# Seven block products for eight in the retention projections of a decoder layer

## The chip, the cores and the metric

The kernel runs on one core of one Trainium2 chip. Five engines work side by side, each with its own queue of instructions, taken in order: TensorE (PE, matrix products), VectorE (DVE), ScalarE (ACT), GpSimd (POOL) and SyncE (SP), which here starts all transfers. The metric is the time of one execution on the device, in microseconds (us); lower is better.

## The reference

One decoder layer with norms after the sums, for 8 batches of 100 tokens of width 1024, all in float32: retention with 8 heads, then attention to a context of 722 tokens per batch and the own tokens, then a gated feed-forward layer. The change touches the retention:

```python
q = (hidden_states @ Wq).reshape(B, T, H, DK)      # H = 8, DK = 128
k = (hidden_states @ Wk).reshape(B, T, H, DK)
v = (hidden_states @ Wv).reshape(B, T, H, DV)      # DV = 256
g = (hidden_states @ Wg).reshape(B, T, H, DV)
q = _rope(q)
k = _rope(k)
...
scores = jnp.einsum('bihd,bjhd->bhij', q * scale, k) * D[None]
o = jnp.einsum('bhij,bjhd->bihd', scores, v)
rms = jax.lax.rsqrt(jnp.mean(o * o, axis=-1, keepdims=True) + EPS)
o = o * rms * g_norm_weight
o = o * (g * jax.nn.sigmoid(g))
return o.reshape(B, T, H * DV) @ Wo
```

## The kernel before

The 800 tokens are worked in two halves of 400 (`N`), with features on the 128 partitions and tokens along the free dimension. A weight block of 1024 x 128 lies as eight 128 x 128 tiles side by side (`KT` = 8), and eight matmuls of 400 columns add up in one PSUM accumulator.

Float32 precision is kept by splitting. `split` writes an operand as a rounded part and a rest: a cast on ScalarE (line 69), then a subtraction on VectorE (line 70). `mm3` (lines 88 to 90) forms one product from three matmuls: high x high, high x low, low x high. `load_w` brings 512 KB of a weight block into a raw tile `wst` (3 buffers) and splits it into a tile `w` (4 buffers). `proj` forms one block for one half: 24 matmuls.

The retention stage first loads x, as pairs of k tiles (`xs`), and splits it into four `big` tiles, two for each half of the tokens, one for each half of the 1024 contraction rows. Then it goes over the 8 heads. A head takes six weight blocks: q, k, two of v and two of the gate. Each of the six is multiplied with both halves. q and k pass through `rope` (VectorE, lines 134 to 137, straight from PSUM). v is copied out by ScalarE and turned by four TensorE transposes (`tokens_first`). Scores (line 349), their decay (350), the products with v (356), the squares and their sums follow. Then a block of the context weights `wc[h]` is split and stored to DRAM for a later stage (`wcd`), the gate blocks are formed and passed through Silu, and `inv_root` with a sum over partitions on GpSimd (`all_red`, line 125) scales the result, which is split into `of` and stored to DRAM (`o1d`). The output projection and layer norm (`out_proj`) follow, which reload `o1d` into the `big` tiles. PSUM has three accumulators with tag `a`, four with `s` and one with `v`.

Later come the second attention and the feed-forward stage. The latter already forms its products in sevens (`seven`, by Strassen's sums), which prepares weight quarters by sums (`w_pair`, line 631), copies products out on ScalarE (line 659) and adds them on VectorE (line 663).

The order in which instructions stand on each engine is not that of the source: a scheduler interleaves independent work when the program is built, within what tiles, buffers and dependences allow. Waits between engines go by semaphores that it sets.

Of the kernel before, what the change touches and what calls it, by code (L numbers as in the profile page):

```python
# [8 lines left out]
F32 = mybir.dt.float32  # L9
# [19 lines left out]
T6 = T - R6            # first token that sees keys of chunk 6  # L29
N6 = 4 * R6            # scores of chunk 6, of the tokens that see its keys  # L30
NH1 = 8                # heads of the first attention
NKV = 4                # kv heads of the second
NHID = 32              # blocks of the hidden width
UNITS = NHID // 2      # pairs of hidden blocks
LAST = 3               # pairs of the last down projection
CUT = 5 * T            # tokens in the first of the two parts that are normed last
# [5 lines left out]
def decoder_layer(ctx, tc, xT, cT, w1, wo1, w2, wo2, wc, w3, wd, gw, qw, kw, trig, dec, mask, out):  # L42
# [21 lines left out]
    def split(dst, src):  # L64
        """dst[:, 0] + dst[:, 1] == src, each with the 12 significant bits that one pass takes."""
        split2(dst[:, 0], dst[:, 1], src)
# [20 lines left out]
    def mm3(acc, lh, ll, rh, rl, start, stop):  # L87
        nc.tensor.matmul(acc, lh, rh, start=start, stop=False)  # L88
        nc.tensor.matmul(acc, lh, rl, start=False, stop=False)  # L89
        nc.tensor.matmul(acc, ll, rh, start=False, stop=stop)  # L90
# [20 lines left out]

    def inv_root(pool, ss, eps, n=N):
        """-2 (ss + eps)^-1/2: by exp(-ln/2), then a Newton step."""
        r = pool.tile([P, n], F32, tag="r0", name="r0")
        nc.scalar.activation(r, ss, AF.Ln, bias=eps)  # L115
        nc.scalar.activation(r, r, AF.Exp, scale=-0.5)  # L116
        q = pool.tile([P, n], F32, tag="r1", name="r1")
        nc.scalar.activation(q, r, AF.Square)
        nc.vector.scalar_tensor_tensor(q, ss, eps, q, ALU.add, ALU.mult)  # L119
        nc.vector.scalar_tensor_tensor(q, q, 3.0, r, ALU.subtract, ALU.mult)  # L120
        return q
# [6 lines left out]
    def rope(pool, acc, cosw, sinw, tag="t1"):  # L128
        """acc * cos + (acc with its halves swapped) * sin."""
# [10 lines left out]
    def tokens_first(pool, acc):  # L140
        """[128, 4 x 100] -> PSUM [100, 4 x 128]: the transposes of the four batches."""
        vt = pool.tile([P, N], F32, tag="vt", name="vt", bufs=1)
        nc.scalar.copy(vt, acc)
        tr = bank("s")
        for b in range(NB):
            nc.tensor.transpose(tr[0:T, b * P:(b + 1) * P], vt[:, b * T:(b + 1) * T], ident)
        return tr[0:T]

# [1 line left out]
    o1d = dr.tile([NH1, P, 2, 2, 2, N], FR, name="o1d")            # head, p, half, block, hi/lo, token  # L150
# [11 lines left out]
    def big(shape):  # L162
        return bp.tile(shape, FR, tag="big", name="big")

# [28 lines left out]
    def load_constants(p, trg):  # L193
# [6 lines left out]
        # rotary tables with the norm weights of q and k; factors left over from inv_root  # L200
# [7 lines left out]
    def out_proj(half, w, load_o, res, yp, ybufs, p, make_z, dst, after=None):  # L208
        """res + o @ w of one half, then its layer norm: split for the next products, and to dst."""
# [71 lines left out]
    # A norm with little left to do once the last block of rows is there: all blocks are taken relative to the mean  # L281
    # of the others, so that the mean of what they then hold, delta, is that of the last block alone, and the
    # variance is mean(y^2) - delta^2 (delta^2 is at most an eighth of mean(y^2)).
# [24 lines left out]
    with sbuf("l1", 2) as p:  # L308
        x = []
        for half in range(2):  # L310
            z = [big([P, 2, QT, N]) for _ in range(2)]
            if half == 0:
                w0 = load_w(w1[0, 0], parts=4)
            for k in range(0, KT, 2):
                xs = p.tile([P, 2, N], F32, tag="xs", name="xs", bufs=4)
                nc.sync.dma_start(out=xs, in_=xT[half, :, k:k + 2])
                for i in range(2):
                    split(z[k // QT][:, :, k % QT + i], xs[:, i])
            if half == 0:
                wk0 = load_w(w1[0, 1])  # L320
                trg = p.tile([P, 4, T], F32, name="trg", bufs=1)
                nc.sync.dma_start(out=trg, in_=trig)
            x.append(z)
        dcy = load_constants(p, trg)

        for h in range(NH1):
            qk = [[None, None], [None, None]]
            for i in range(2):
                w = (w0, wk0)[i] if h == 0 else load_w(w1[h, i])
                for half in range(2):  # L330
                    t = rope(p, proj(w, x[half]), trg[:, 2 * i], trg[:, 2 * i + 1], f"qk{i}")
                    qk[i][half] = t
            v = [[None, None], [None, None]]
            for blk in range(2):
                w = load_w(w1[h, 2 + blk])
                for half in range(2):
                    tr = tokens_first(p, proj(w, x[half]))
                    vv = p.tile([T, NB * P], F32, tag=f"v{blk}", name="vv")
                    nc.scalar.copy(vv, tr)
                    v[half][blk] = vv  # L340
            # scores with their decay, and o^T
            oo, sq = [[None, None], [None, None]], [[None, None], [None, None]]
            for half in range(2):
# [7 lines left out]
                for blk in range(2):  # L351
# [6 lines left out]
                    s_ = p.tile([P, N], F32, tag=f"sq{blk}", name="sq")  # L358
# [4 lines left out]
            # a block of the context weights, split once for all batches  # L363
            w = load_w(wc[h])
            nc.sync.dma_start(out=f32(wcd[h]), in_=f32(w))
            wg = [load_w(w1[h, 4 + blk]) for blk in range(2)]
            g = [[None, None], [None, None]]
            for half in range(2):
                for blk in range(2):
                    gs = p.tile([P, N], F32, tag=f"g{blk}", name="gs")  # L370
                    nc.scalar.activation(gs, proj(wg[blk], x[half]), AF.Silu)
                    g[half][blk] = gs
            ln_exp()
            for half in range(2):
                r = inv_root(p, all_red(p, sq[half][0], "ss"), eps_o)
                for blk in range(2):
# [3 lines left out]
                    of = p.tile([P, 2, N], FR, tag="of", name="of")  # L380
# [46 lines left out]
    y2pool = sbuf("y2", 1)  # L427
    y2p = y2pool.__enter__()
    with sbuf("cx", 2) as p, sbuf("c1", 1) as p1:
        for b in range(B):  # L430
# [10 lines left out]
            for kv in range(NKV):  # L441
                # K^T of the context, to be scaled by its norms when the scores leave PSUM, and V
# [29 lines left out]
                # -2 / norm of the context keys, keys on partitions  # L472
# [14 lines left out]
                # scores, keys on partitions, and their maximum  # L487
# [23 lines left out]
                # exponentials, split, and their sum  # L511
# [27 lines left out]
                # 1 / sum: exp(-ln), then a Newton step (the sum is 1 or more)  # L539
# [22 lines left out]
    # [C11 C12; C21 C22] = [A11 A12; A21 A22] [B11 B12; B21 B22] by Strassen's seven products; the rows of A  # L562
    # are two blocks of one weight, the columns of B the two halves of the tokens
# [53 lines left out]
    H = QT * P  # L617

    def load_raw(src):
        st = wp.tile([P, KT * P], F32, tag="wst", name="wst", bufs=3)  # L620
        nc.sync.dma_start(out=st, in_=src)
        return st

    def w_pair(*ops):
        """Two of the sums of quarters of a weight, split; a sum goes to the first quarter's place unless that is kept."""
# [15 lines left out]
    def seven(i, part, t0=None):  # L641
        """Two blocks of the gate (part 0) or of the other factor (part 1): C11, C12, C21, C22."""
# [24 lines left out]
        add(s2, s2, s4)                                     # C21  # L667
# [6 lines left out]
        add(s4, s4, prod(t2, 1, "b11+b12"))                 # C22  # L674
        m5 = prod(t3, 0, "b22")
        add(s1, s1, m5, ALU.subtract)                       # C11
        add(s3, s3, m5)                                     # C12
        return s1, s3, s2, s4

    # the first two blocks by all eight products: half of them need the first half of the tokens alone  # L680
# [13 lines left out]
    with sbuf("ff", 1) as p:  # L694
# [59 lines left out]
        # the last rows are normed in two parts  # L754
# [16 lines left out]
def _chunks(w, n):  # L771
    """[K, M] -> [M / 128, K / (n 128), 128, n 128]: k tiles of 128 x 128 side by side."""
# [66 lines left out]
```

## Time and profile before

| | us |
|---|---|
| median of 3 runs | 2617.55 (2616.77 to 2619.95) |
| span of the profiled execution | 2615.0 |
| TensorE busy in it | 2552.7 (98%) |
| VectorE busy | 1922.2 (74%) |
| ScalarE busy | 1256.3 (48%) |
| GpSimd busy | 466.3 (18%) |
| matmuls | 14438 |

The span reaches from the first to the last instruction of the one execution that was profiled; the page gives no other time for that execution, and the median of the timed runs lies 2.55 us above its span. The retention stage takes about the first 500 us. Group rows read: line, engine, operation, written tile <- read tiles, shapes and count | busy us, mean ns of one | idle time before them and what ended it. Matmuls overlap each other, so the mean of one is longer than the distance between two starts. A row of windows gives the busy us of each engine in a stretch, with the number of instructions, the granted TensorE clock, the busy share of the DMA engines and GB/s.

### The profile page before, as it was taken

The page shows a single profiled execution, that of the slowest core. Times are in us where ns is not written, and L with a number is a line of the kernel's source. Part 1 is how long each engine was busy: PE and PEld are TensorE (multiplying, and loading weights), DVE is VectorE, ACT ScalarE, POOL GpSimd, SP SyncE. Part 2 cuts the span into 40 slices and gives each one's busy share as a digit, 9 for nine tenths or more (in the row PEclk, how much of TensorE's full clock was granted, in tenths as well). Part 3 has the DMA queues.
Part 4 walks back from the last instruction along what each step waited for, and adds up shares of the span by engine and source line. Part 5 has one row for each costly group of instructions (what it writes and reads, how often), then busy time and mean ns, then how long its engine had stood idle before and what let it go on. Part 6 is the DMA issues. An engine that isn't in the chain of part 4 may idle for free.

```text
span 2615.0 us, 37589 instructions
## 1 busy us (share of the span) xinstructions
PE 2552.7 (98%) x14438; PEld 2511.4 (96%) x14438; DVE 1922.2 (74%) x3201; ACT 1256.3 (48%) x2202; POOL 466.3 (18%) x222
## 2 busy tenths in 40 slices
PE   8999999999998899999999999999999999999998
PEld 8999999999998899999999999999999999999996
DVE  4454554456999888888988989866866766866885
ACT  4555544533555455655655566533433433423351
POOL 0010000000544434434333343100000000000000
PEclk9999999999999999999999999999999999999999
DMA  5323333664434644544554553564421211211221
GB/s 173 98 98 119 100 117 122 214 241 154 144 133 138 236 158 137 188 158 146 174 166 139 185 173 113 210 245 143 146 73 65 73 57 65 81 50 64 70 84 51
DMA packets 157233, 346.44 MB, mean 132 GB/s; under 512 B 45018, under 2 KB 95578, under 8 KB 147838
## 3 DMA queue, kind: packets, MB, share of 16 engines
q1 hardware_dynamic: 157054, 344.05, 39.5%
q8 instruction: 113, 1.85, 0.3%
q14 instruction: 66, 0.54, 0.1%
HBM read 279.81 MB, written 64.19 MB: 132 GB/s over the span
## 4 chain that ended last, share of the span: by engine, by line
PE 80%; DVE 10%; ACT 6%; issue 3%; DMA 2%; SPq 0%; DVEq 0%; ACTq 0%
PE a L88 16%; PE a L90 16%; PE a L89 16%; PE s L88 8%; PE s L89 8%; PE s L90 8%; PE v L88 3%; PE v L90 2%; PE v L89 2%; DVE r L119 1%; ACT L116 1%; ACT L115 1%; PE s L469 1%; DVE ot L378 1%; DVE t L136 1%
## 5 line engine op out<-in xcount | busy, mean ns | idle before, releaser
L88 PE MATMUL a<-big,w 128*128 128x400 f32 (+2 forms) x2300 | 778.5, 339 | 17.1 <-ACT big L69 9.5
L89 PE MATMUL a<-big,w 128*128 128x400 f32 (+2 forms) x2300 | 779.7, 339 | 0.0
L90 PE MATMUL a<-big,w 128*128 128x400 f32 (+2 forms) x2300 | 778.3, 339 | 0.0
L88 PEld LDWEIGHTS a<-big,w 128*128 128x128 f32 x2300 | 432.4, 188 | 20.6 <-ACT big L69 9.8
L90 PEld LDWEIGHTS a<-big,w 128*128 128x128 f32 x2300 | 433.9, 189 | 0.6
L89 PEld LDWEIGHTS a<-big,w 128*128 128x128 f32 x2300 | 433.1, 188 | 1.1 <-DVE big L70 0.5
L69 ACT CAST w<-wst 128x1024 fp32r<-128x1024 f32 (+2 forms) x300 | 259.2, 869 | 346.6 <-PE a L90 152.6
L70 DVE TENSOR_TENSOR w<-wst,w 128x1024 fp32r<-128x1024 f32 (+2 forms) x300 | 303.7, 1015 | 164.8 <-ACT w L69 163.2
L125 POOL PARTITION_ALL_REDUCE ss<-sq x56 | 157.3, 2817 | 725.4 <-DVE sq L362 442.3
L459 POOL PARTITION_ALL_REDUCE kss<-ksq x64 | 171.6, 2682 | 141.2 <-ACT ksq L458 140.7
L69 ACT CAST w<-as 128x512 fp32r<-128x512 f32 x90 | 55.9, 621 | 215.3 <-PE a L90 180.9
L88 PE MATMUL s<-big,w 128*128 128x400 f32 x428 | 150.4, 352 | 2.5 <-ACT big L69 2.5
L89 PE MATMUL s<-big,w 128*128 128x400 f32 x428 | 149.4, 349 | 1.6 <-DVE big L70 1.6
L90 PE MATMUL s<-big,w 128*128 128x400 f32 x428 | 148.8, 348 | 0.0
L505 ACT ACTIVATE s<-s,rk 128x400 f32<-128x400 f32 x160 | 88.0, 591 | 97.3 <-DVE sm L527 63.3
L663 DVE TENSOR_TENSOR s<-s 128x400 f32<-128x400 f32 x183 | 102.4, 569 | 25.3 <-ACT s L659 19.5
L125 POOL PARTITION_ALL_REDUCE mb<-sm x32 | 83.3, 2603 | 201.1 <-DVE sm L527 201.1
L524 ACT ACTIVATE s<-s 128x800 f32<-128x800 f32 (+1 forms) x128 | 95.1, 750 | 41.0 <-DVE s L518 38.1
L70 DVE TENSOR_TENSOR pl<-s,ph 128x800 fp32r<-128x800 f32 (+1 forms) x128 | 108.3, 850 | 2.5 <-ACT ph L69 2.0
L506 DVE TENSOR_TENSOR mx<-mx,s 128x400 f32<-128x400 f32 x128 | 80.5, 629 | 26.5 <-ACT s L505 23.3
L88 PE MATMUL a<-z,w 128*128 128x400 f32 x192 | 70.5, 367 | 24.0 <-DVE t L136 22.9
L69 ACT CAST ph<-s 128x800 fp32r<-128x800 f32 (+1 forms) x128 | 92.4, 731 | 0.9
(269 smaller groups left out, 5605.6 us busy)
## 6 DMA issues: line engine op xcount, KB each, us to landing
wst<-in_w SPq DMA_DIRECT2D x137, 512.0 KB
w<-wcd SPq DMA_DIRECT2D x64, 1024.0 KB
wst<-in_wo SPq DMA_DIRECT2D x64, 512.0 KB
wst<-in_wd SPq DMA_DIRECT2D x32, 512.0 KB
o1d<-of SPq DMA_DIRECT2D x32, 400.0 KB
big<-o1d SPq DMA_DIRECT2D x16, 800.0 KB
qd<-d SPq DMA_DIRECT2D x32, 400.0 KB
q<-qd SPq DMA_DIRECT2D x32, 400.0 KB
```

Of the source, the lines that this page charges most:

```text
L69: nc.scalar.copy(hi, src)
L70: nc.vector.tensor_tensor(lo, src, f32(hi), ALU.subtract)
L88: nc.tensor.matmul(acc, lh, rh, start=start, stop=False)
L89: nc.tensor.matmul(acc, lh, rl, start=False, stop=False)
L90: nc.tensor.matmul(acc, ll, rh, start=False, stop=stop)
L115: nc.scalar.activation(r, ss, AF.Ln, bias=eps)
L125: nc.gpsimd.partition_all_reduce(y, x, P, op)
L459: nc.gpsimd.partition_all_reduce(ss[:, at], sq[:, at], P, RED.add)
L505: nc.scalar.activation(sc, sp, AF.Copy, scale=rk[:, c:c + 1])
L506: nc.vector.tensor_tensor(mx, s[:, 1] if j == 2 else mx, sc, ALU.max)
L524: nc.scalar.activation(e, e, AF.Exp)
L663: nc.vector.tensor_tensor(t, x, y, op)
```

## The change

The two weight blocks of a pair (q and k, the two of v, the two of the gate) are taken as two rows of a 2 x 2 block matrix, whose columns are the two halves of the contraction. x is the other 2 x 2 block matrix: rows are the contraction halves, columns the token halves. The four blocks of the product then take seven block products, in the Winograd form of Strassen's method, for eight. For head 0, q and k stay as they were.

Four differences of the quarters of x (`t1` to `t4`) are formed and split once, from a second load of x. `t1`, `t2` and `t3` get tiles of their own; `t4` takes the `big` tile of quarter b12, which the seven products don't read. For each pair, four sums of weight quarters are formed on VectorE, and 3 1/2 tiles of split weights for two. Some products add onto an accumulator that already holds an earlier one, after ScalarE has copied out that earlier one; three sums on VectorE finish the blocks. One of the four blocks of a pair stays in PSUM, so three of the four copies ahead of the transposes go.

Besides, x is loaded in blocks of one k tile into a pool of ten tiles `tp`, which also holds the copied products; the sum over partitions moves ahead of the gate; the squares `sq` and the tile `of` get one buffer for two. Apart from removed comments, the rest is unchanged.

```diff
+    def wino_weights(pool, src0, src1):
+        r0, r1 = load_raw(src0), load_raw(src1)
+        a11, a12, a21, a22 = r0[:, :H], r0[:, H:], r1[:, :H], r1[:, H:]
+        ta = w_split(r0)
+        v = pool.tile([P, 2 * H], F32, tag="ws", name="ws", bufs=1)
+        nc.vector.tensor_tensor(v[:, :H], a21, a22, ALU.add)
+        nc.vector.tensor_tensor(a21, a11, a21, ALU.subtract)
+        tb = w_split(r1)
+        nc.vector.tensor_tensor(a11, v[:, :H], a11, ALU.subtract)
+        td = w_split(a11)
+        nc.vector.tensor_tensor(v[:, H:], a12, a11, ALU.subtract)
+        return dict(A11=(ta, 0), A12=(ta, 1), S3=(tb, 0), A22=(tb, 1), S2=(td, 0)), v
+
+    def wino(pool, src0, src1, zb, temp, tags):
+        w, v = wino_weights(pool, src0, src1)
+        x, y, z = (bank(t)[:, :N] for t in tags)
...
+        prod(x, "A11", "b11")
+        p1 = copied(x)
+        prod(y, "S3", "t3")
+        p7 = copied(y)
+        prod(x, "S2", "t2", start=False)
+        u2 = copied(x)
+        prod(z, "A12", "b21")
+        nc.vector.tensor_tensor(p1, z, p1, ALU.add)
+        tc_ = w_split(v)
+        w["S1"], w["S4"] = (tc_, 0), (tc_, 1)
+        prod(x, "S1", "t1", start=False)
+        nc.vector.tensor_tensor(p7, x, p7, ALU.add)
+        prod(y, "A22", "t4", start=False)
+        nc.vector.tensor_tensor(u2, y, u2, ALU.add)
+        prod(x, "S4", "b22", start=False)
+        return p1, x, u2, p7
...
+        qk0 = [[proj(w, x[half]) for half in range(2)] for w in (w0, wk0)]
+        for name in ("t1", "t2", "t3"):
+            zb[name] = p.tile([P, 2, QT, N], FR, tag="zt", name=name, bufs=3)
+        zb["t4"] = big([P, 2, QT, N])
+        for k in range(QT):
+            r = {}
+            for name, half, kk in (("b11", 0, k), ("b12", 1, k), ("b21", 0, QT + k), ("b22", 1, QT + k)):
+                r[name] = temp()
+                nc.sync.dma_start(out=r[name], in_=xT[half, :, kk])
+            def mixed(name, dst, a, b):
+                nc.vector.tensor_tensor(r[dst], r[a], r[b], ALU.subtract)
+                split(zb[name][:, :, k], r[dst])
...
+            mixed("t3", "t3", "b22", "b12")
+            mixed("t1", "b12", "b12", "b11")
+            mixed("t2", "b22", "b22", "b12")
+            mixed("t4", "b21", "b21", "b22")
...
-            for i in range(2):
-                w = (w0, wk0)[i] if h == 0 else load_w(w1[h, i])
-                for half in range(2):
-                    t = rope(p, proj(w, x[half]), trg[:, 2 * i], trg[:, 2 * i + 1], f"qk{i}")
-                    qk[i][half] = t
+            for half, i in ((0, 0), (1, 1), (0, 1), (1, 0)):
+                qk[i][half] = rope(p, acc[i][half], trg[:, 2 * i], trg[:, 2 * i + 1], f"qk{i}")
+            c11, c12, c21, c22 = wino(p, w1[h, 2], w1[h, 3], zb, temp, "asa")
...
+                ss.append(all_red(p, sq[half][0], "ss"))
...
-            wg = [load_w(w1[h, 4 + blk]) for blk in range(2)]
+            c11, c12, c21, c22 = wino(p, w1[h, 4], w1[h, 5], zb, temp, "asa")
...
-                    of = p.tile([P, 2, N], FR, tag="of", name="of")
+                    of = p.tile([P, 2, N], FR, tag="of", name="of", bufs=1)
```

More of the change, by code (lines that the diff above doesn't have):

```diff
@@ L85, in load_ws, with mm3 @@
         return w
[L87 to L90, printed above, removed]
+    def mm3(acc, lh, ll, rh, rl, start, stop, chain=False):
+        nc.tensor.matmul(acc, lh, rh, start=start, stop=False, skip_group_check=chain)
+        nc.tensor.matmul(acc, lh, rl, start=False, stop=False, skip_group_check=chain)
+        nc.tensor.matmul(acc, ll, rh, start=False, stop=stop, skip_group_check=chain)
     def mmw(acc, w, k, rh, rl, start, stop):
@@ L138, in rope, with tokens_first @@
         return t1
-    def tokens_first(pool, acc):
-        vt = pool.tile([P, N], F32, tag="vt", name="vt", bufs=1)
-        nc.scalar.copy(vt, acc)
+    def tokens_first(pool, acc, copied=True):
+        vt = acc
+        if copied:
+            vt = pool.tile([P, N], F32, tag="vt", name="vt", bufs=1)
+            nc.scalar.copy(vt, acc)
         tr = bank("s")
@@ L305, in norm_late, with load_raw, w_split @@
         scaled(y, r, dst, z)
+    H = QT * P
+    def load_raw(src):
+        st = wp.tile([P, KT * P], F32, tag="wst", name="wst", bufs=3)
+        nc.sync.dma_start(out=st, in_=src)
+        return st
+    def w_split(src):
+        w = wp.tile([P, 2, KT * P], FR, tag="w", name="w", bufs=4)
+        split(w[:, :, :src.shape[1]], src)
+        return w
+    def wino_weights(pool, src0, src1):
[10 more added lines that the diff above has]
+        return dict(A11=(ta, 0), A12=(ta, 1), S3=(tb, 0), A22=(tb, 1), S2=(td, 0)), v
@@ new lines, in wino, with prod, copied @@
+    def wino(pool, src0, src1, zb, temp, tags):
+        w, v = wino_weights(pool, src0, src1)
+        x, y, z = (bank(t)[:, :N] for t in tags)
+        def prod(acc, a, b, start=True, stop=True):
+            t, c = w[a]
+            for k in range(QT):
+                e = slice(c * H + k * P, c * H + (k + 1) * P)
+                mm3(acc, t[:, 0, e], t[:, 1, e], zb[b][:, 0, k], zb[b][:, 1, k],
+                    start and k == 0, stop and k == QT - 1, True)
+        def copied(acc):
+            t = temp()
+            nc.scalar.copy(t, acc)
+            return t
+        prod(x, "A11", "b11")
[14 more added lines that the diff above has]
+        return p1, x, u2, p7
@@ L308, in decoder_layer, with temp @@
     with sbuf("l1", 2) as p:
-        x = []
+        def temp():
+            return p.tile([P, N], F32, tag="tp", name="tp", bufs=10)
+        zb = {}
         for half in range(2):
-            z = [big([P, 2, QT, N]) for _ in range(2)]
+            zb["b1%d" % (half + 1)], zb["b2%d" % (half + 1)] = big([P, 2, QT, N]), big([P, 2, QT, N])
             if half == 0:
                 w0 = load_w(w1[0, 0], parts=4)
-            for k in range(0, KT, 2):
-                xs = p.tile([P, 2, N], F32, tag="xs", name="xs", bufs=4)
-                nc.sync.dma_start(out=xs, in_=xT[half, :, k:k + 2])
-                for i in range(2):
-                    split(z[k // QT][:, :, k % QT + i], xs[:, i])
+            for k in range(KT):
+                xs = temp()
+                nc.sync.dma_start(out=xs, in_=xT[half, :, k])
+                split(zb["b%d%d" % (k // QT + 1, half + 1)][:, :, k % QT], xs)
@@ L322, in decoder_layer @@
                 nc.sync.dma_start(out=trg, in_=trig)
-            x.append(z)
+        x = [[zb["b11"], zb["b21"]], [zb["b12"], zb["b22"]]]
         dcy = load_constants(p, trg)
-        for h in range(NH1):
-            qk = [[None, None], [None, None]]
-            for i in range(2):
-                w = (w0, wk0)[i] if h == 0 else load_w(w1[h, i])
-                for half in range(2):
-                    t = rope(p, proj(w, x[half]), trg[:, 2 * i], trg[:, 2 * i + 1], f"qk{i}")
-                    qk[i][half] = t
-            v = [[None, None], [None, None]]
[L334 to L342, printed above, removed]
+        qk0 = [[proj(w, x[half]) for half in range(2)] for w in (w0, wk0)]
@@ new lines, in decoder_layer @@
+        for name in ("t1", "t2", "t3"):
+            zb[name] = p.tile([P, 2, QT, N], FR, tag="zt", name=name, bufs=3)
+        zb["t4"] = big([P, 2, QT, N])
+        for k in range(QT):
+            r = {}
[5 more added lines that the diff above has]
+                split(zb[name][:, :, k], r[dst])
+            t3 = temp()
+            r["t3"] = t3
+            mixed("t3", "t3", "b22", "b12")
+            mixed("t1", "b12", "b12", "b11")
+            mixed("t2", "b22", "b22", "b12")
+            mixed("t4", "b21", "b21", "b22")
@@ new lines, in decoder_layer @@
+        for h in range(NH1):
+            if h == 0:
+                acc = qk0
+            else:
+                c11, c12, c21, c22 = wino(p, w1[h, 0], w1[h, 1], zb, temp, "asa")
+                acc = [[c11, c12], [c21, c22]]
+            qk = [[None, None], [None, None]]
+            for half, i in ((0, 0), (1, 1), (0, 1), (1, 0)):
+                qk[i][half] = rope(p, acc[i][half], trg[:, 2 * i], trg[:, 2 * i + 1], f"qk{i}")
+            c11, c12, c21, c22 = wino(p, w1[h, 2], w1[h, 3], zb, temp, "asa")
+            v = [[None, None], [None, None]]
+            for half, blk, c in ((0, 0, c11), (1, 1, c22), (0, 1, c21), (1, 0, c12)):
+                tr = tokens_first(p, c, half == 1 and blk == 0)
+                vv = p.tile([T, NB * P], F32, tag=f"v{blk}", name="vv")
+                nc.scalar.copy(vv, tr)
+                v[half][blk] = vv
+            oo, sq, ss = [[None, None], [None, None]], [[None, None], [None, None]], []
@@ L357, in decoder_layer @@
                     nc.scalar.copy(ot, o)
-                    s_ = p.tile([P, N], F32, tag=f"sq{blk}", name="sq")
+                    s_ = p.tile([P, N], F32, tag=f"sq{blk}", name="sq", bufs=1)
                     nc.scalar.activation(s_, ot, AF.Square)
@@ L362, in decoder_layer @@
                 nc.vector.tensor_tensor(sq[half][0], sq[half][0], sq[half][1], ALU.add)
+                ss.append(all_red(p, sq[half][0], "ss"))
             w = load_w(wc[h])
             nc.sync.dma_start(out=f32(wcd[h]), in_=f32(w))
-            wg = [load_w(w1[h, 4 + blk]) for blk in range(2)]
+            c11, c12, c21, c22 = wino(p, w1[h, 4], w1[h, 5], zb, temp, "asa")
             g = [[None, None], [None, None]]
[L368 to L372, printed above, removed]
+            for half, blk, c in ((0, 0, c11), (1, 1, c22), (0, 1, c21), (1, 0, c12)):
+                gs = temp() if c is c12 else c
+                nc.scalar.activation(gs, c, AF.Silu)
+                g[half][blk] = gs
             ln_exp()
             for half in range(2):
-                r = inv_root(p, all_red(p, sq[half][0], "ss"), eps_o)
+                r = inv_root(p, ss[half], eps_o)
                 for blk in range(2):
@@ L615, in next_bank @@
         return bank("aaassssv"[ring[0] % 8])[:, :N]
[L617 to L622, printed above, removed]
     def w_pair(*ops):
```

## The prediction

> **What bounds the kernel now.** I read the page's engine totals first, then the stretches of the retention stage one head at a time, then the waits of TensorE there, then the groups that hold the nearest relatives of the new instructions.
>
> ```profile
> PE 2552.7 (98%) x14438; PEld 2511.4 (96%) x14438; DVE 1922.2 (74%) x3201; ACT 1256.3 (48%) x2202; POOL 466.3 (18%) x222
> ```
> ```profile
> core 0: us, PE busy (x) PEld busy (x) DVE busy (x) ACT busy (x) POOL busy (x), PEclk, DMA share, GB/s
> 39.86:100.18 60.32, 59.47 (x355) 58.99 (x353) 29.59 (x43) 31.70 (x45) 5.47 (x2) 1.00 0.34 111
> 100.18:160.50 60.32, 59.49 (x355) 59.00 (x353) 29.24 (x44) 31.70 (x45) 5.46 (x2) 1.00 0.32 106
> ```
> ```profile
> PE a L88 <- DVE t L136: 7.4, 8, 1.6
> ```
> The second view cuts at the same transpose of successive heads: one head lasts 60.3 us, TensorE works 59.5 of it, VectorE 29.4, ScalarE 31.7. In all the stage TensorE waits only 7.4 us, for the rotary step to give back an accumulator. So a head is TensorE's work plus about 0.85 us, and matmuls removed are time removed as long as the half-idle engines can feed the rest.
>
> ```profile
> 1900.00:1960.00 60.00, 60.00 (x331) 59.98 (x331) 39.95 (x71) 18.40 (x33) 0.00 (x0) 1.00 0.18 62
> ```
> This stretch of the feed-forward stage, where nearly all matmuls are 128x400, prices one: 60.00 / 331 = 0.1813 us.
>
> **What is removed.** A pair of weight blocks times two token halves took 2 x 2 x 8 x 3 = 96 matmuls and takes 7 x 4 x 3 = 84. There are 23 pairs (three per head; the q and k of head 0 stay as they are), so 23 x 12 = 276 go; the built order of TensorE shows just that, 4552 to 4460 on each of the three matmul lines. 276 x 0.1813 = 50.0 us: 6.53 in each of heads 1 to 7, 4.35 in head 0.
>
> **What is added in a head, and what hides it.** The prices:
>
> ```profile
> L663 DVE TENSOR_TENSOR s<-s 128x400 f32<-128x400 f32 x87 | 48.9, 570 | 7.7 <-ACT s L659 6.0 <-PE s L90 1.5
> L631 DVE TENSOR_TENSOR wst<-wst 128x512 f32<-128x512 f32 x30 | 20.6, 687 | 0.2
> L70 DVE TENSOR_TENSOR w<-wst,w 128x1024 fp32r<-128x1024 f32 x14 | 17.1, 1225 | 5.4 <-ACT w L69 5.4
> ```
> ```profile
> L69 ACT CAST w<-wst 128x512 fp32r<-128x512 f32 x60 | 36.9, 621 | 31.5 <-PE s L90 14.0 <-PE a L90 7.0 <-PE v L90 7.0
> L659 ACT COPY s<-a 128x400 f32<-128x400 f32 x19 | 9.4, 493 | 19.3 <-PE a L90 19.1
> L69 ACT CAST w<-wst 128x1024 fp32r<-128x1024 f32 x14 | 14.7, 1050 | 11.7 <-issue 7.6 <-ACT s L701 2.1 <-ACT s L659 1.0
> ```
> VectorE, per pair: splits of three whole weights and a half for two wholes, 1.225 + 0.687 = 1.91; four sums of weight quarters, 4 x 0.687 = 2.75; three sums of products, 3 x 0.570 = 1.71. That is 6.4, or 19.1 a head: 29.4 becomes 48.5. ScalarE, per pair: casts 1.050 + 0.621, three copies at 0.493, 3.15 in all, 9.45 a head; less three copies of accumulators before the transposes (1.5) and one table load (1.28): 31.7 becomes 38.4. The new head is 60.3 - 6.5 = 53.8 us, so VectorE would be 90% busy, ScalarE 71%. What such a load does to TensorE stands in two other stages:
>
> ```profile
> 820.00:880.00 60.00, 50.95 (x273) 50.25 (x272) 59.49 (x87) 33.58 (x64) 25.84 (x10) 0.96 0.54 184
> 1540.00:1600.00 60.00, 60.00 (x359) 58.57 (x358) 57.76 (x98) 37.84 (x71) 21.83 (x12) 1.00 0.59 195
> ```
> At 96% (second row) TensorE has no gap; at 99% (first row) it loses 9 us in 60. 90% lies on the good side, so I put the new VectorE and ScalarE work at nothing. If the cover goes, each us by which VectorE's work and waits exceed 53.8 is paid seven times.
>
> Four things could take that cover. (1) A pair now takes four split-weight tiles, and there are still four: a split waits until TensorE is done with an older tile. The shortest hand-over I find in the built order is from the value pair to the gate pair: 24 matmuls, 4 scores and 4 transposes, 24 x 0.1813 + 0.35 + 0.44 = 5.1 us, against two casts, a split and a split's tail of 1.05 + 1.05 + 1.22 + 0.6 = 3.9 us. It holds by 1.2 us. Behind a late split stand, on VectorE, the sums that give accumulators back and, on ScalarE, the copies that the next product into the same accumulator needs. (2) Products now accumulate onto an accumulator that ScalarE has copied out (three a pair). In the order at least 21 matmuls, 3.8 us, lie between such a product and its successor; the copy needs 0.5. (3) The output tile `of` has one buffer for two, so its cast waits for the store of the one before; a copy for TensorE is next in ScalarE's queue. No row shows the store's time; two reloads of 800 KB took about 8 us from issue, so 400 KB is between 1 and 4 us, and I take 4; TensorE's cover is 34 matmuls, 6.2 us. (4) The two partition sums move ahead of the gate. They take GpSimd 2.7 us each as before, with most of the gate's products as cover; nothing. Together they cost between -0.85 us a head (the rotary wait goes as well) and +3; I take nothing, since each cover holds on paper. SP's queue has the same loads of weights a head, in the same order: nothing.
>
> **The start.** x is loaded a second time (16 blocks of 200 KB), and four differences of its quarters are formed and split, before the value pair of head 0 can end. Before, the first value matmul runs here:
>
> ```profile
> 29.14 0.34 PE L90 MATMUL a<-big,w 128*128 128x400 f32 x1
> 31.05 0.42 PE L88 MATMUL a<-big,w 128*128 128x400 f32 x1 [1.56 <-DVE t L136]
> ```
> ```profile
> 0.00:30.00 30.00, 19.98 (x96) 18.96 (x96) 17.80 (x41) 14.44 (x25) 0.69 (x6) 1.00 0.75 253
> ```
> At 253 GB/s, what SP issues up to and including the value weights (x 3.3 MB, q and k weights 1.05, tables 0.6, four blocks of x again 0.8, value weights 1.05: 6.8 MB) has landed at about 28 us. The order then has seven VectorE steps to the first weight difference (to 31.0) and a cast of 1.05 ahead of TensorE's next matmul: 32.2, only 1 us late. But from there VectorE has 49 instructions in front of the last difference of x: 38 of 400 columns, 7 of 512, 4 of 1024 (rotary, weight sums and splits lie between): 38 x 0.57 + 7 x 0.687 + 4 x 1.225 = 31.4 us, so 62.4. TensorE's order has 84 matmuls up to the last that needs it; they fit inside, and the 180th matmul of the program ends near 63. Before, the 180th ends at 31.05 + 84 x 0.1813 plus 1.1 for scores and transposes, 47.4. So TensorE stands for 15.6 us in head 0. Lower end: the same instructions back to back (0.5, 0.6 and 1.13 us from start to start in the timeline) take 27.7, so 11.9. Upper end: the value weights 4 us later (6.8 MB at 220 GB/s), 20, and three cold restarts, 28:
>
> ```profile
> 680.66 0.34 PE L90 MATMUL s<-z,w 128*128 128x400 f32 x1
> 685.16 0.67 PE L88 MATMUL a<-z,w 128*128 128x400 f32 x1 [4.16 <-DVE t L136]
> 685.63 0.54 PE L89 MATMUL a<-z,w 128*128 128x400 f32 x1
> ```
> After this wait of 4.16 us the next 17 matmuls start 0.333 us apart, not 0.181: 2.6 us lost. After the 1.56 us wait above they do not. The walk has one wait of that length in head 0 (27 to 32 us), and its 2.6 us fall while VectorE is the later one; so I charge nothing for it, and 2.6 apiece if later waits grow as long. The Trainium skill ("TensorE: Matmul & The Clock Gate", Part 1) has it that an idle window of about 3.4 us halves the clock until such a window has been busy; by that, an estimate, each long wait would cost half of one window, 1.7 us, and the upper end above would be 2.7 us lower.
>
> **The end of the stage.** The output projection needs head 7's reload. The order leaves 109 matmuls, 19.8 us, between the last gate product and the first use, against 8 us for the reload: nothing, at worst 5.
>
> **Sum.** -50.0 + 15.6 = -34.4 us. Against the profiled execution that is a span of 2615.0 - 34.4 = 2580.6; the median lies 2.55 above that span, so 2583.
>
> **Rivals.**
> - *As summed* (0.48): start 11.9 to 20, heads within +1 and -0.85 us: 2573 to 2595.
> - *Start nearly free, rotary wait gone* (0.12): -50.0 - 5.9 + 6: 2568. For it: TensorE has other products to pull forward, and the order does so. Against: two thirds of them need the same VectorE.
> - *Hand-overs miss* (0.20): each pair waits 1 us, 3 a head: -34.4 + 21 gives 2604. For it: the margin of 1.2 us. Against: 87 to 96% on VectorE leaves no gap in the context stage.
> - *Slower: VectorE's queue, in order, becomes the bound* (0.16). The place is the row of splits and sums of each pair: each split waits for a cast, each cast for a freed tile, and the sums behind them hold TensorE. The point where it decides: head 0 loses 15.6 - 4.35 = 11.25 us, so the other seven must each be 1.6 shorter, 58.7 us, which is 48.5 of work and 10.2 of waits on VectorE. With 12.5 of waits, 61.0 us, it gives 2617.5 + 11.3 + 7 x 0.7 = 2634. For it: at 99% in the row above, VectorE does hold TensorE. Against: there its work fills the time; here 90% would.
> - *No change* (0.04): the same with heads near 58.7. That the matmuls do not go is excluded by the order.
>
> A difference under 0.2%, 5 us, cannot be told from none. Faster is the first three, 0.80; same 0.04; slower 0.16. The range of eight in ten leaves out the last two: 2563 (all gains, start free to 1 us) to 2612.
>
> **What would show it.** Right: heads of 53 to 55 us between like transposes, with 319 matmuls each for 355; VectorE near 48 us in each; TensorE gaps of about 15 us between 27 and 65 us, ended by VectorE or ScalarE. Wrong: heads above 57 with TensorE waiting on splits or copies; a gap over 25 us at the start; gaps ahead of the output projection; the clock below 1.00 after head 0.

## The result: slower by 0.8%, and the profile after

The change makes the kernel slower: median 2639.14 us (2637.20 to 2640.34, 4 runs) against 2617.64 us for the kernel before on the same chip, a ratio of 1.0079 with a 95% interval of 1.0065 to 1.0093. I had predicted 2583 and a range that ended at 2612.

The page's engine totals, and the row of windows for one head, cut at the same transposes of heads 1 and 2 (columns as before):

```profile
PE 2532.9 (96%) x14162; PEld 2484.6 (94%) x14162; DVE 2063.2 (78%) x3440; ACT 1315.8 (50%) x2301; POOL 463.7 (18%) x222
```
```profile
127.55:189.50 61.95, 56.43 (x318) 55.30 (x316) 44.94 (x70) 37.66 (x56) 5.21 (x2) 0.92 0.31 105
```

The 276 matmuls are gone (14438 to 14162; 318 in this head for 355), and TensorE's share of the span fell from 98% to 96%. But the head is 62 us long, not 53.8, and the granted clock in it is 0.92. VectorE works 44.9 us of it and ScalarE 37.7, both less than the 48.5 and 38.4 that I had reckoned. (I had added up whole durations, and neighbours overlap: between 149.41 and 150.87 in the timeline VectorE's instructions of 0.57 us start 0.48 to 0.49 us apart.) So neither engine is full, and still TensorE waits. Its waits over heads 1 to 7 (us in total, times, longest):

```profile
PE a L88 <- DVE tp L369: 21.6, 7, 3.1
PE a L88 <- ACT tp L355: 17.0, 7, 2.6
```

Once a head TensorE waits for a sum of products (line 369) and once for a copy of a product (355), 5.5 us together. Before, its only wait in a head was the rotary step's, some 0.8 us. The chain of waits through one head shows what the sum and the copy were waiting for (start, us, what):

```profile
137.68 1.07 ACT sq L448 x2
138.77 1.28 ACT L115
...
143.91 1.28 ACT L115
145.20 0.64 ACT r L115
...
146.36 1.28 ACT L116
...
149.98 0.48 DVE r L120
150.47 0.49 DVE tp L369
151.00 0.70 PE a L88
151.70 0.33 PE a L89
...
155.93 1.28 ACT L110
157.22 0.50 ACT tp L355
157.77 0.70 PE a L88
```

Lines 115 and 116 are the logarithm and the exponential of the head's norm; rows of 1.28 us without a tile are ScalarE's table loads, of which a head has seven. From 137.7 to 150.5 us the chain runs through the norm. The sum of line 369 had its product by 146.3 (the last matmul of that product starts at 146.08 in the timeline). It ran at 150.38, because VectorE's queue had the second half of the norm in front of it, which waits for ScalarE. Then the copy: the last matmul of the next pair's first product starts at 139.16, and the copy started at 157.22, because in ScalarE's queue the head's last Silu, which waits for TensorE's last product, and a table load stood before it. Behind each wait the next matmuls start 0.33 us apart for 0.18 (the first step is 0.50): 12 after the first, 8 after the second, about 3.4 us more.

The last transposes of head 0 stand at 55.03 us in the timeline of before and at 71.08 in that of after, those of head 7 at 477.14 and 502.67. Head 0 ends its values 16.1 us later. The seven heads from there take 431.6 us for 422.1, so 61.66 each for 60.30, together +9.5. Everything behind takes 2135.3 for 2137.9, -2.5. The sum is the 23.0 us by which the span grew (2615.0 to 2638.0).

### The profile page after: what moved, and what is told of

Read it like the earlier page. It is cut to its first block, busy times and chain, and to the rows that moved or that the text cites. A ratio compares the mean times of both kernels' runs of the same rounds, so it can differ in the third digit from the quotient of the medians.

```text
span 2638.0 us, 37487 instructions
## 1 busy us (share of the span) xinstructions
PE 2532.9 (96%) x14162; PEld 2484.6 (94%) x14162; DVE 2063.2 (78%) x3440; ACT 1315.8 (50%) x2301; POOL 463.7 (18%) x222
## 4 chain that ended last, share of the span: by engine, by line
PE 81%; DVE 9%; ACT 5%; issue 3%; DMA 2%; SPq 0%; DVEq 0%; ACTq 0%
PE a L88 16%; PE a L89 15%; PE a L90 15%; PE s L88 8%; PE s L89 8%; PE s L90 8%; PE v L88 3%; PE v L90 2%; PE v L89 2%; PE s L445 1%; DVE r L119 1%; DVE w L70 1%; ACT L116 1%; ACT L115 1%; PE s L558 1%
## 5 line engine op out<-in xcount | busy, mean ns | idle before, releaser
L88 PE MATMUL a<-big,w 128*128 128x400 f32 (+2 forms) x1840 | 627.2, 342 | 30.1 <-DVE tp L369 22.1
L89 PE MATMUL a<-big,w 128*128 128x400 f32 (+2 forms) x1840 | 624.3, 339 | 0.0
L90 PE MATMUL a<-big,w 128*128 128x400 f32 (+2 forms) x1840 | 622.2, 340 | 0.9 <-DVE w L70 0.9
L69 ACT CAST w<-wst 128x1024 fp32r<-128x1024 f32 (+2 forms) x323 | 274.0, 852 | 269.3 <-PE a L90 121.9
L70 DVE TENSOR_TENSOR w<-wst,w 128x1024 fp32r<-128x1024 f32 (+2 forms) x323 | 319.5, 992 | 81.0 <-ACT w L69 79.5
L88 PEld LDWEIGHTS a<-big,w 128*128 128x128 f32 x1840 | 349.7, 190 | 34.7 <-DVE tp L369 24.8
L90 PEld LDWEIGHTS a<-big,w 128*128 128x128 f32 x1840 | 350.4, 191 | 2.1 <-DVE w L70 1.5
L89 PEld LDWEIGHTS a<-big,w 128*128 128x128 f32 x1840 | 350.6, 191 | 1.3 <-DVE big L70 0.6
L88 PE MATMUL s<-big,w 128*128 128x400 f32 x520 | 182.6, 352 | 2.5 <-ACT big L69 2.5
L89 PE MATMUL s<-big,w 128*128 128x400 f32 x520 | 181.4, 349 | 1.8 <-DVE big L70 1.8
L90 PE MATMUL s<-big,w 128*128 128x400 f32 x520 | 180.4, 348 | 0.9 <-DVE w L70 0.9
L69 ACT CAST w<-as 128x512 fp32r<-128x512 f32 x90 | 55.9, 621 | 218.3 <-PE a L90 181.0
L88 PEld LDWEIGHTS s<-big,w 128*128 128x128 f32 x520 | 99.2, 191 | 4.8 <-ACT big L69 3.9
L89 PEld LDWEIGHTS s<-big,w 128*128 128x128 f32 x520 | 99.1, 191 | 3.5 <-DVE big L70 2.6
```

Of the source, the lines that this page charges most:

```text
L69: nc.scalar.copy(hi, src)
L70: nc.vector.tensor_tensor(lo, src, f32(hi), ALU.subtract)
L88: nc.tensor.matmul(acc, lh, rh, start=start, stop=False, skip_group_check=chain)
L89: nc.tensor.matmul(acc, lh, rl, start=False, stop=False, skip_group_check=chain)
L90: nc.tensor.matmul(acc, ll, rh, start=False, stop=stop, skip_group_check=chain)
```

## The experiments

Theory A: the accumulators come back late because their copies and sums stand, in two queues that are taken in order, behind the norm of the same head and its table loads; the load on VectorE is not the reason. Theory B: VectorE's new work, with the splits and the four tiles of split weights, has become the bound, so that no order of the queues helps. The column "head" is the mean of heads 1 to 7, from the last transposes of head 0 to those of head 7.

| kernel | median, us | ratio to before (95%) | head, us |
|---|---|---|---|
| before | 2617.64 | | 60.30 |
| after | 2639.14 | 1.0079 (1.0065 to 1.0093) | 61.66 |
| norm behind the gate | 2614.09 | 0.9985 (0.9976 to 0.9995) | 58.37 |
| no tables | 2600.76 (one run) | | 56.07 |
| copies and sums first | 2614.89 | 0.9988 (0.9979 to 0.9998) | 58.52 |
| value 0 by eight | 2623.72 | 1.0021 (1.0010 to 1.0031) | 62.23 |
| order and copies | 2596.85 | 0.9923 (0.9906 to 0.9939) | 55.86 |
| the same, value 0 by eight | 2590.06 | 0.9897 (0.9882 to 0.9911) | 56.13 |
| last Silu behind the copies | 2596.18 | 0.9914 (0.9900 to 0.9929) | 57.29 |
| value copy first as well | 2604.64 | 0.9945 (0.9929 to 0.9962) | 56.84 |
| before, norm behind the gate | 2608.78 | 0.9968 (0.9955 to 0.9981) | 59.23 |

**Norm behind the gate.** Only the order changes: the two halves of the norm are issued after the last Silu.

```diff
...
-            ln_exp()
+            pre = ln_exp()
+            with tc.issue_after(pre.ins):
+                rr_ = [inv_root(p, ss[half], eps_o) for half in range(2)]
             for half in range(2):
-                r = inv_root(p, ss[half], eps_o)
+                r = rr_[half]
```

> Edit: in each retention head the logarithms, exponentials and squares of both halves' norm are queued on ScalarE behind the table load that stands after the gate's Silus. By the order built, ScalarE then loads 2 activation tables a head instead of 7, and VectorE's sum ahead of the gate's last product is no longer behind the norm's second half. Theory A (ScalarE's queue: the norm's chain of table loads holds a sum on VectorE and a copy on ScalarE that TensorE waits for; a head of the changed kernel lasts 61.95 us, of which waits are 5.5 and matmuls at half rate after them about 3): the wait for the sum (3.1 us) goes, the wait for the copy stays or grows to 3.6 us, since two logarithms now stand ahead of it; head 57 to 59.7 us, time 2604 to 2623 us. Theory B (VectorE's load of about 48 us a head and the hand-over of four weight tiles hold TensorE): neither is touched, 2639 +- 5 us.

2614.09, 25 us off, with the same matmuls, splits and sums, and two table loads a head for seven. TensorE's waits in heads 1 to 7:

```profile
PE a L88 <- ACT tp L355: 23.9, 7, 3.4
PE a L90 <- DVE w L70: 3.0, 3, 1.0
PE a L88 <- DVE tp L369: 0.5, 1, 0.5
```

The wait for the sum is gone. The wait for the copy has grown, from 2.4 to 3.4 us, since the two logarithms now stand between the last Silu and the copy. So the order of ScalarE's queue, with five table loads a head fewer in it, set the time, and not VectorE's load, which speaks against theory B; but the edit has put more work in front of the copy.

**No tables.** The norm's logarithm becomes Identity and its exponential a scaled Copy, which need no load of their own; the reciprocal root is left out.

```diff
...
-                r = inv_root(p, ss[half], eps_o)
+                r = inv_root(p, ss[half], eps_o, f1=AF.Identity, f2=AF.Copy, scale=1e-9)
```

> Edit: the logarithm and the exponential of the retention's norm are replaced by an identity and a scaled copy, which need no table of their own; this leaves out the reciprocal root. The order on the engines is nearly that of the changed kernel, with 2 table loads a head for 7 (6.4 us of ScalarE less). Theory A: the wait for the sum goes and with it the half-rate matmuls; the wait for the copy behind the one table load after the Silus stays at 2.4 us; head about 56 us, time about 2597 us. Theory B: 2639 +- 5 us.

2600.76, from a kernel whose norm leaves out the root. With the instructions of VectorE as they were, the wait for the sum goes (0.9 us once in seven heads, for 21.6), and that for the copy stays at 2.4 a head, as the last Silu is still in front of it (heads 1 to 7):

```profile
PE a L88 <- ACT tp L355: 16.8, 7, 2.4
PE a L88 <- DVE tp L369: 0.9, 1, 0.9
```

**Copies and sums first.** The copies and sums of the seven products get priority in the built order; the seven table loads stay.

```diff
-            nc.scalar.copy(t, acc)
+            with tc.high_priority():
+                nc.scalar.copy(t, acc)
...
-        nc.vector.tensor_tensor(p1, z, p1, ALU.add)
+        add(p1, z, p1)          # the same sum, with priority; likewise for p7 and u2
...
```

> Edit: the copies and sums of the products get priority when the order on the engines is made; no instruction is added or removed, the 7 table loads a head stay. By the order built, the sum ahead of the gate's last product stands before the second half of the norm, and the copy that the next pair waits for stands before the table load after the Silus. Theory A: the wait for the sum goes, the wait for the copy shrinks from 2.4 to 1.2 us, few matmuls at half rate; head 54.7 us, time about 2588 us. Theory B: same load on VectorE and the same tiles, 2639 +- 5 us.

2614.89, half of the gain that I expected. The waits show why (heads 1 to 7; with this edit the copies stand on line 356 and all the sums on line 361):

```profile
PE a L88 <- ACT tp L356: 15.5, 7, 4.0
PE a L88 <- DVE tp L361: 12.0, 6, 3.1
```

TensorE still waits for the sum in six heads of seven. On VectorE the norm's second half still precedes it: in the timeline of head 2's gate VectorE waits 1.39 us for ScalarE at line 119 and comes to the sum 1.5 us later. Why priority did not take the sum past it in the built order I did not find out. The copy is prompt there (a wait of 1.0 us, at 212.4). But in two heads it is waited for longer than ever, 4.0 and 3.7 us: in the first of them the cast of the norm's output, which waits for VectorE, runs at 150.43 in ScalarE's queue, ahead of the last Silu and of the copy at 151.25.

**Value 0 by eight.** The values of head 0 are formed by eight products, and the four differences of x are traced behind them.

```diff
-            c11, c12, c21, c22 = wino(p, w1[h, 2], w1[h, 3], zb, temp, "asa")
+            if h > 0:
+                c11, c12, c21, c22 = wino(p, w1[h, 2], w1[h, 3], zb, temp, "asa")
+            else:
+                wv0 = [load_w(w1[0, 2 + blk]) for blk in range(2)]
+                c11, c21, c12, c22 = [proj(wv0[blk], x[half]) for half in range(2) for blk in range(2)]
+                differences()
...
```

> Edit: the two value blocks of head 0 are formed by eight products as well, so that the differences of x are first needed by its gate. 12 matmuls more (2.2 us). If VectorE's steps for the differences are what TensorE stood for at the start (15.6 us by the prediction's walk), this gives 15.6 - 2.2 = 13 us back: 2626 us, with heads 1 to 7 unchanged at 61.9 us. If the second load of x, or the rest of the start, is the cause, less than 4 us come back.

2623.72, 15.4 us off, and both waits of every head stay (3.1 and 2.4). But the trace does not bear out the reason in full. Head 0's last transposes come at 61.95 for 71.08, and head 7's at 497.54 for 502.67: 5 us of the 15 are won in the stage. The first reload of the residual, some 400 us further on, is at 898.4 for 911.9, so 8 us came off between the two, in work that the edit does not touch. That stretch takes 401 to 419 us in the traces of these runs. Most of the 8 us can be placed: behind the stage TensorE waits for the rotary step (line 136) 23.5 us in the changed kernel and 14.3 here, and one wait of 7.2 us, some 330 us behind head 7's transposes, is missing. It is missing too in the runs with the norm behind the gate, with order and copies and with value 0 by eight on top; it is there in the kernel before, in the control and in the run with the copies and sums first alone. Why the built order has it in the one and not in the other I did not follow.

**Order and copies.** The first and the third edit together.

> Both edits together: the logarithms and exponentials of the head's norm stand behind the last Silu (2 table loads a head for 7), and the copies and sums of the seven products are put ahead of ready work in their queues. Matmuls and VectorE's work stay as in the changed kernel. Theory A (TensorE stands because its accumulators come back late, from copies and sums that wait in ScalarE's and VectorE's queues behind the norm and its table loads): both waits of a head go; what is left is at most 1.2 us for the copy of the next pair; the norm-behind-gate run left 25 us of copy waits and some 70 matmuls at half rate in 8 heads (70 x 0.15 = 10 us), so 2614 - 25 - 10 + 5 = 2584, heads of 53.5 to 55 us. Rival B (VectorE at 48.5 us of work in a head of 53.5 is itself the bound, whatever the order): another wait takes their place, heads stay at 57 or more and the time above 2605.

2596.85, heads of 55.86, and the granted clock 1.00 in every stretch of 60 us from 60 to 480. The waits of heads 1 to 7:

```profile
PE a L88 <- ACT tp L356: 6.8, 7, 1.0
PE s L148 <- ACT vt L145: 4.3, 5, 1.2
PE a L90 <- DVE w L70: 4.2, 8, 0.6
PE a L88 <- DVE t L136: 3.8, 7, 0.5
```

Neither edit alone had brought more than 25 us; together they bring 42, since the one had left the wait in ScalarE's queue, and the other more than half of that in VectorE's and nearly all of that in ScalarE's. What is left is 2.8 us a head in pieces of 1.2 us or less; VectorE works 44.0 us in a head of 55.9, for 44.8 of 61.7 in the changed kernel (means of heads 1 to 7), so it is fuller, and TensorE waits less. The median is 13 us above theory A's figure and 8 below theory B's bound.

**The same, with value 0 by eight.** All three edits.

> The run before, and besides the values of head 0 by 8 products with the differences of x formed behind them. If the start and the heads are separate losses, the 15.4 us that this gave back alone come off again: 2565 to 2575. If the differences, moved later, now compete with head 1's sums and splits, since heads are shorter, less than 8 us come off.

2590.06, the fastest version of this study, but 6.8 us off the run before, not 15.4. Of the 10 us that head 0 wins (60.81 for 70.88), 8 are left at head 7 (453.75 for 461.90), and 6 at the end. So the lower branch of the expectation came true, though not for its reason: head 1 gives back only 2 to 3 us. The other 8 us that value 0 by eight had shown came from the stretch behind the stage, and that takes 408 us in both of these runs, as both are without the long rotary wait.

**Last Silu behind the copies, and value copy first as well.** The Silus, the norm and the output of a head are traced inside the next head's q and k pair, behind its first two copies. The second run also puts the copy ahead of the values' transposes first.

```diff
...
+        if between is not None:     # the Silus, norm and output of the head before
+            between()
         prod(x, "S2", "t2", start=False)
         u2 = copied(x)
...
```

> The run with value 0 by eight, and besides the Silus, the norm and the output of a head are traced inside the next head's q and k pair, behind its first two copies, so that on ScalarE the copy that the pair's second product into its first accumulator needs stands ahead of the last Silu, which waits for the head's last product. Theory A: the copy waits, 6.8 us in the stage in the run before, go; 2590 - 7 = 2583, heads of 55.2 us. Rival: the waits only pass on to the next reader of the queue (the transposes' copy, the rotary step): 2587 to 2593.

> The same, with the copy ahead of the values' transposes put first in ScalarE's queue too. Theory A: its waits, 3.2 us in the stage, go as well: 2580. Rival: nothing changes, within 2 us of the run beside it.

2596.18 and 2604.64: both slower than the run without them. For the first the ratios alone do not settle it, since their intervals overlap; its heads do, 57.29 us for 56.13. In it the copy waits are gone, all of them, and this stands in their place (heads 1 to 7):

```profile
PE a L88 <- ACT w L69: 9.2, 6, 2.3
```

Casts of weights are late now, by up to 2.3 us, splits behind them 4.5 us more in six waits, and the clock is at 0.94 to 0.97 in three of the stretches. The rival was right in kind and too mild in size: something else in the same queue paid. In the worst case the cast runs at 372.97, and ahead of it in ScalarE's queue stand the last Silu (at 370.11, as soon as TensorE's product is there), a table load and the two logarithms. In the second run TensorE waits no more in heads 1 to 7 for the copies ahead of the transposes, and 6.8 us for casts. Its heads are shorter than those of the first, 56.84 us; what makes it slower is the part behind head 7's transposes, 2144.6 us for 2131.4, where the long rotary wait is back with 8.5 us.

**Before, norm behind the gate.** The control: the order edit on the kernel before.

> The kernel before, with the logarithms and exponentials of the norm held behind the last Silu of the head, as in the norm-behind-gate run. Theory A: before the change no accumulator waits on a copy or a sum behind the norm; TensorE waits 7.4 us in the whole stage, so 2612 to 2619. Rival C (grouping the table loads is worth some 3 us a head in any kernel, and says nothing of the change): 2590 to 2600.

2608.78, a gain of 9 us where I expected at most 6; heads of 59.23, with no wait of TensorE in heads 1 to 7 at all. So a part of the order's gain was to be had without the change. With it in both, seven products for eight are worth 2608.78 - 2596.85 = 12 us, and 19 with the start mended. By the traces the 12 are 23.6 us won in heads 1 to 7, 16.5 lost in head 0 and 4.7 won behind, where the control has the long rotary wait.

## Why the prediction was wrong

**The removed matmuls: right.** 276 went, and with the order mended the heads show it: the control has 59.23 us of TensorE's work without a wait, so 59.23 - 6.53 = 52.70 is what a head could be.

**The heads: the step that failed is "I put the new VectorE and ScalarE work at nothing", and in it the second cover, the products that accumulate onto copied accumulators.** I compared 0.5 us for the copy with 3.8 us of matmuls, as if a copy ran when its product was ready. It ran 18 us later (139.2 to 157.2). The other wait, for the sum of line 369, is of a hand-over that none of the four covers counted: a pair's last product adds onto an accumulator that this sum has to read first, and in the gate pair only 8 matmuls (146.26 to 147.54), 1.45 us, lie between. At 0.57 us a sum that ran when its product was ready would have fitted; it ran 4 us later. Nor do the 21 matmuls hold everywhere: in heads 0 and 1 there are hand-overs with 3, 14, 16 and 20 between. I also took 90% of load on VectorE for the measure. The load was lower than that, 44.9 of 62 us, and meant nothing: what held TensorE was the order of two queues. The head comes out as 52.70 + 5.5 of waits + about 3.4 for matmuls at half rate = 61.6, measured 61.66: heads above 57 with TensorE waiting on copies, as I had named the sign of being wrong. Against my 53.8 that is 7.86 x 7 = 55.0 us, nearly all of the 57.4 by which the span missed 2580.6.

The profile of before had the evidence, in two views that I did not use for this. VectorE's waits in the stage (first view), and the chain of one head of before, from Silu to the accumulator that TensorE waits for:

```profile
DVE r L119 <- ACT r L118: 95.3, 16, 9.0
```
```profile
62.53 0.50 ACT gs L371
63.05 1.28 ACT L115
...
78.66 1.28 ACT L371
...
86.28 0.58 DVE t L136
87.00 0.42 PE a L88
```

VectorE already stood 12 us a head at line 119, and anything queued behind it stood too. And a second chain, 24.5 us long, ran through the norm, its table loads and the rotary step to TensorE, and came out 0.8 us behind TensorE's own work. I read that wait as a small loss that would go. It could have been read as a chain without slack: take work from TensorE and the chain is what remains, and the change hung new links, the sums and copies, onto it. The control shows the same from the other side: with the norm moved, the kernel before loses its wait.

**The other covers held.** (1) In the changed kernel no weight tile comes late in heads 1 to 7. (Where the last Silu went behind the copies, casts did come late, but from what stood before them in ScalarE's queue.) (3) ScalarE waits for the store behind `of` 12 times, up to 4.2 us, as I feared, but it is not the wait in the chain. It is so in the order-and-copies run at the end of the stage: there a store of 4.6 us, a cast with its subtraction, a store of 2.3 us and a reload of 4.9 us follow one another up to the first matmul of the output projection. (4) The partition sums cost nothing: the norm starts 8 us behind a head's last transposes in both kernels (63.05 for 55.03 before, 138.77 for 130.61 after).

**The clock: "charge nothing" was wrong.** I had read a price of 2.6 us from one wait of 4.16 us and would charge it only for waits "as long". Waits of 2.4 to 3.1 us, twice a head, were enough; they cost 2.0 and 1.4 us in the head shown, 3.4 together.

**The start: right.** In the first 60 us TensorE did 194 matmuls; it had done 276. These are the windows of before and after:

```profile
0.00:60.00 60.00, 48.93 (x276) 47.76 (x277) 30.58 (x58) 26.22 (x43) 1.00 (x7) 1.00 0.56 188
```
```profile
0.00:60.00 60.00, 41.37 (x194) 37.68 (x195) 49.56 (x98) 28.83 (x48) 0.73 (x6) 0.91 0.64 208
```

82 x 0.1813 = 14.9 us, against the 15.6 I had walked. Its make-up differs: between 27 us and the last transposes TensorE's waits are 11.4 us, not 15, and some 3 us are matmuls at half rate, which I had charged at nothing here too.

**The end of the stage: right** for this kernel (-2.5 us behind head 7's transposes, of which 2.2 are the 12 matmuls that its gate pair saves). In five of the faster versions the output projection waits 4.9 to 7.4 us for the reload, more than the "at worst 5" of the prediction in most.

**The rivals.** The slower one, at 0.16, had the mechanism half right: a queue in order, decided at 58.7 us a head, and 12.5 us of waits for a head of 61.0 and 2634. Its place was wrong. It was not the row of splits and casts but the norm, and ScalarE's queue as much as VectorE's. So that its 2634 came within about 5 us of the measured time is in part luck. I gave it little because the row at 99% load seemed to be its only support.

**What stays open**: why some of these built orders have the long rotary wait behind the stage and others not. Whether the seven products can be fed without the 2.8 us a head of short waits is open too; two attempts to remove them moved them.

## What to carry to other kernels

When work is taken off the busiest engine, follow the second chain through the same stage and see how little it is behind: a wait of 0.8 us at the end of a chain of 24 us says that the chain is level with the engine, not only that 0.8 us are lost. Cost a new copy or sum that hands an accumulator back by what stands in front of it in its queue, and by what those instructions wait for, not by its duration or by the load of its engine. And when two queues hold the same engine up, mending one shows little.

## What the runs showed of the hardware

A change of ScalarE's table took 1.28 us each time, and the next instruction started at its end (143.91 and 145.20 in the chain). The Trainium skill ("ScalarE: Activation LUTs", section "What ACT_TABLE_LOAD costs") has the same figure for the load and adds a drain of about 1.38 us to each switch; in this place no such time is to be seen, as the load at 138.77 starts 0.02 us after the squares end.

A wait of 2.4 us can be enough to halve TensorE's rate. In the run without tables the same wait of 2.4 us, once a head, was followed by 8 matmuls or more at 0.33 us in four heads and by none in three; after waits of 3.1 us slow matmuls always came, and after the single waits of 1.2 us or less of the order-and-copies run never. The Trainium skill ("TensorE: Matmul & The Clock Gate", Part 1) speaks of an idle window of about 3.4 us that runs freely; that the same wait sometimes counts and sometimes doesn't fits a free-running window, but the threshold in these runs lies below that length.
